# Where the sums for a Winograd aggregate are made: on GpSimd while the rows are at hand, or on VectorE from rows read back

## The chip, the cores and the metric

The kernel runs on one core of a Trainium2 chip. The metric is the device time of one execution in microseconds (us). The kernel before takes 3149.56 us, the median of three runs from 3143.49 to 3149.83 us; one further execution, taken with the hardware profiler, has a span of 3144.7 us, and its trace is what is read below.

## The reference, cut to what matters

Two graph layers on N = 2708 nodes with 1024 features. Only layer 0 is touched.

```python
h = jnp.maximum(_layernorm(x, axis=-1), 0.0)          # 2708 x 1024
f = h @ Wf + bf
g = h @ Wg + bg
e = relu(f @ g.T)
scores = where(adj > 0, e, NEG)                         # adj: 2708 x 2708 int32
attention = softmax(scores, axis=1)
x = x + (attention @ h) @ W + bW                        # the kernel's order of the two products
# layer 1: the same shape, with leaky_relu(f1 + f2.T) for e
```

So `h` is wanted twice: transposed, for the scores, and by rows, as one side of `attention @ h` ("the aggregate").

## The kernel before

Every large product is made by a Winograd form of Strassen's scheme: seven products of half-size blocks instead of eight. Each side of each product is a block or a sum of blocks. For the aggregate the row side is made of pairs of row tiles (a, b), each cut into two halves of 512 columns: `ha[0], ha[1], hb[0], hb[1]`. Seven operands come of it, stored in HBM as `hg_d[layer][group][:, m, j]`, with `m` in the order M1, M5, M6, M7, M3, M2, M4:

- M1, M2, M4 are plain halves: `ha[0]`, `hb[0]`, `hb[1]`;
- M5 = ha[1] + hb[1], M6 = M5 - ha[0], M7 = ha[0] - ha[1], M3 = hb[0] - M6 are sums.

Ten such pairs cover 20 of the 22 tiles. In the setup, while the products of the weights occupy TensorE, each pair is loaded, normalized, transposed, and:

```python
def stream(name, shape=(P, D), dt=FP):           # 12 buffers of 512 KB, for everything that streams
    return strm.tile(list(shape), dt, tag="strm", name=name)

def load(o, i):                                   # all loads: one queue (SyncE), kept in program order
    for a, b in in_16(o, i):
        tc.keep_in_program_order(nc.sync.dma_start(a, b))

def store(o, i):                                  # all stores: GpSimd's queue
    for a, b in in_16(o, i):
        nc.gpsimd.dma_start(a, b)

def pair_h(l, q, ha, hb):
    n = P
    on = nc.vector if l else nc.gpsimd
    g1, g2 = stream("g1", (P, 2, W)), stream("g2", (P, 2, W))
    s1, s2, s3, s4 = g1[:n, 0], g1[:n, 1], g2[:n, 0], g2[:n, 1]
    on.tensor_tensor(s1, ha[1], hb[1], OP.add)
    on.tensor_tensor(s2, s1, ha[0], OP.subtract)
    on.tensor_tensor(s3, ha[0], ha[1], OP.subtract)
    on.tensor_tensor(s4, hb[0], s2, OP.subtract)
    i, j = group_of[q]
    for m, h in ((M1, ha[0]), (M2, hb[0]), (M4, hb[1])):
        store(hg_d[l][i][:n, m, j], h)
    store(hg_d[l][i][:n, M5:M6 + 1, j], g1[:n])
    store(hg_d[l][i][:n, M7:M3 + 1, j], g2[:n])
```

Pieces of work that lie beside others are put on a list and taken from it a few at a time, `rate` us of estimated work after each product; what the next pieces load is fetched when they are among the first five of the list:

```python
later, credit = [], [0.0]
ahead = [5]
def put(us, go, fetch=None, takes_psum=False, ready=None): ...
def one():
    for it in later[:ahead[0]]:
        if it[1]:
            it[1]()                                # the fetch
            it[1] = None
    us, _, go = later.pop(0)[:3]
    go()
    return us
def behind(us, psum_free=False): ...               # one() until the credit is used up
```

After the weights' product M and the projection "q" of panel 0 come the first scores. For each pair q of ten, seven products of four matmuls each; the transposed operands are read from HBM, two products' worth per load, and the int32 adjacency for the pair after the next is fetched in eight small DMAs and made into a mask by VectorE:

```python
def product(q, m, ps, start):
    n, i = P, BY_SCORES.index(m)
    if i % 2 == 0:
        t = stream("As", (P, 2, NH, P))
        lefts[q] = t
        k = min(2, 7 - i)
        load(t[:, :k]..., hs_d[q][:, i:i + k]...)
    for c in range(NH):
        nc.tensor.matmul(ps[:n, :h], lefts[q][:, i % 2, c, :n], B[m][c // 2][:, c % 2, :h], ...)

nc.hold = ("vector",)                              # VectorE in program order during the scores
for q in range(NQ):
    make_until(q + 2)
    rate = 1.3 if NQ - 1 not in made else rates[p]      # rates[0] = 0.6
    if q + 2 <= LEFT:
        fetch(q + 2)                               # adj_i: stream("adj_i"), four DMAs; adj_t: four more
    ...
    product(q, M1, X, True)
    for s in (lo, hi):
        add(m1[:n, s], X[:n, :h], rb[:n, s])       # VectorE empties PSUM
    if left_over:
        left_over()                                # product M4 of the pair before
    product(q, M6, Z, True)
    add(t[:n, lo], Z[:n, :h], m1[:n, hi])
    behind(rate, True)
    ...                                            # M5, M2, M7, M3 alike; convert and turn the mask
```

The last pairs' normalization, transposes and sums for the scores run on into these first scores. The aggregate of panel 0 comes after the softmax and reads `hg_d`, 512 KB per load, into the same stream buffers.

Of the kernel before, what the change touches and what calls it, by code (L numbers as in the profile page):

```python
# [18 lines left out]
P = 128  # L19
W = 512  # L20
# [5 lines left out]
M1, M5, M6, M7, M3, M2, M4 = range(7)  # L26
# [31 lines left out]
def kernel(  # L58
# [19 lines left out]
    nc = InOrder(tc)  # L78
# [31 lines left out]
    NQ = len(pairs)  # L110
    pair_of = {t: (t // 2, t % 2) for t in range(MONO)}
    LEFT = NQ
# [15 lines left out]
    def stream(name, shape=(P, D), dt=FP):  # L128
        return strm.tile(list(shape), dt, tag="strm", name=name)

    def in_16(o, i):

        n = o.shape[0]
        k = n // 16 * 16
        return [(o, i)] if n in (k, 1) or not k or i.shape[0] != n else [(o[:k], i[:k]), (o[k:], i[k:])]

    def load(o, i):
        for a, b in in_16(o, i):
            tc.keep_in_program_order(nc.sync.dma_start(a, b))  # L139

    def store(o, i):
        for a, b in in_16(o, i):
            nc.gpsimd.dma_start(a, b)  # L143
# [11 lines left out]
    group_of = {q: (i, j) for i, g in enumerate(groups) for j, q in enumerate(g)}  # L155
    assert sorted(group_of) == list(range(NQ))
    hg_d = [[dram.tile([P, 7, len(g), W], FP, name=f"hg{l}_d{i}") for i, g in enumerate(groups)] for l in range(2)]
# [27 lines left out]
    def put(us, go, fetch=None, takes_psum=False, ready=None):  # L185
        later.append([us, fetch, go, takes_psum, ready])
# [4 lines that stand above are left out]
                it[1]()  # L191
# [4 lines that stand above are left out]
# [46 lines left out]
    def add(o, a, b):  # L242
        nc.vector.tensor_tensor(o, a, b, OP.add)

    def sub(o, a, b):
        nc.vector.tensor_tensor(o, a, b, OP.subtract)
# [42 lines left out]
    def left_h(l, hm, ht):  # L289

        for e in range(2):
            store(hgl_d[l][:, e, :W], hm[e])
            for d in range(NH):
                g = slice(B32 * d, B32 * (d + 1))
                store(hgl_d[l][g, e, W:], ht[e][g, d * P:(d + 1) * P])

    def pair_h(l, q, ha, hb):

        n = P
        on = nc.vector if l else nc.gpsimd  # L300
        g1, g2 = stream("g1", (P, 2, W)), stream("g2", (P, 2, W))
        s1, s2, s3, s4 = g1[:n, 0], g1[:n, 1], g2[:n, 0], g2[:n, 1]
        on.tensor_tensor(s1, ha[1], hb[1], OP.add)
# [5 lines that stand above are left out]
            store(hg_d[l][i][:n, m, j], h)  # L309
        store(hg_d[l][i][:n, M5:M6 + 1, j], g1[:n])  # L310
        store(hg_d[l][i][:n, M7:M3 + 1, j], g2[:n])

    u = consts.tile([P, NC], FP, name="u")
    v = consts.tile([P, NC], FP, name="v")
# [5 lines left out]
    def make_pairs():  # L320
        xs, hT = {}, {}

        def fetch(q):
            xs[q] = []
            for t in units[q]:
                xs[q].append(row_halves("x"))
                load_rows_of(t, xs[q][-1], x)

        def rows(q):
            left_h(0, *xs[q]) if q == LEFT else pair_h(0, q, *xs[q])  # L330

        def turned(q, k, e):
            t = units[q][k]
            ps = bank("h_ps", (P, NH, P))
            for c in range(NH):
                nc.tensor.transpose(ps[:, c, :], xs[q][k][e][:, c * P:(c + 1) * P], ident)
            for i, (s, n) in enumerate(pieces[0]):
                if s == t:
                    o = first_h[e].rearrange("p (c i) -> p c i", c=NH)[:, :, i * P:i * P + n]
                    nc.vector.tensor_copy(o, ps[:, :, :n])  # L340
            return ps

        def transposes(q):
            if q == LEFT:
                two = stream("hsl", (P, 2, NH, P))
                for e in range(2):
                    nc.scalar.copy(two[:, e], turned(q, 0, e))
                    nc.scalar.copy(tinyT[:, e], turned(q, 1, e)[:, :, :B32])
                store(hsl_d.rearrange("p e c j -> p (e c j)"), two.rearrange("p e c j -> p (e c j)"))
            else:  # L350
                ts = [stream("hsT", (P, 2, NH, P)) for _ in range(4)]
                hT[q] = ts, lambda i: ts[i // 2][:, i % 2]
                for k, e, i in ((0, 0, 0), (0, 1, 3), (1, 0, 7), (1, 1, 6)):
                    nc.scalar.copy(hT[q][1](i), turned(q, k, e))
            turned_tiles.update(units[q])

        def sums(q):
            if q == LEFT:
                return
            ts, i = hT.pop(q)  # L360
            at = {m: i(k) for k, m in enumerate(BY_SCORES)}
            add(at[M5], i(7), at[M4])
            sub(at[M6], at[M5], at[M1])
            sub(at[M7], at[M1], i(7))
            sub(at[M3], at[M2], at[M6])
            for g, t in enumerate(ts):
                store(hs_d[q][:, 2 * g:2 * g + 2].rearrange("p m c j -> p (m c j)"), t.rearrange("p m c j -> p (m c j)"))

        def dots(q, k):
            t = units[q][k]  # L370
            c = col_of[t]
            dot(r_[:, c:c + 1], xs[q][k], [vb[e][:, :W] for e in range(2)], c0)
            if t == MONO:
                nc.gpsimd.dma_start(r_[:NM, HALF:HALF + 1], r_[NM:, c:c + 1])

        def drop(q, what):
            seen.setdefault(q, set()).add(what)
            if len(seen[q]) == 3:
                xs.pop(q)

        def last(q):
            sums(q)
            drop(q, "sums")
            made.add(q)

        def bias(q, k):
            dots(q, k)
            drop(q, f"dots{k}")

        seen = {}  # L390
        def put_norms(q):
            put(2.1, lambda: normalize(xs[q][0]), lambda: fetch(q))
            put(2.1, lambda: normalize(xs[q][1]))

        put_rows = lambda q: put(0.5, lambda: rows(q))
        def put_dots(q):
            for k in range(2):
                put(1.6, lambda k=k: bias(q, k), ready=lambda: vb[0] is not None)

        todo = [0, 1, LEFT] + list(range(2, NQ))  # L400
        put_norms(todo[0])
        for i, q in enumerate(todo):
            if i + 1 < len(todo):
                put_norms(todo[i + 1])
            put_rows(q)
            put(0.5, lambda q=q: transposes(q), takes_psum=True)
            if i > 1:
                put_dots(q)
            put(2.7 if q != LEFT else 0.0, lambda q=q: last(q))
            if i == 1:  # L410
                put_dots(todo[0])
                put_dots(todo[1])

    def make_until(q):
        while min(q, NQ - 1) not in made:
            one()
# [110 lines left out]
    for name, gs in (("pick_lo", (0, 1)), ("pick_hi", (0, 2, 3))):  # L527
        t = consts.tile([P, P], FP, name=name)
# [228 lines left out]
        return r  # L757

    exps, LAG = [0], 2

    def exps_until(n):
        while exps[0] < n:
# [572 lines left out]
    for p in range(NP):  # L1335
        got["S"], got["acc"] = scores(p, B)
        generated[p] = NQ + 1
        ahead[0] = 2
        S = got["S"]
        hooks = {M1: lambda p=p: take_max(p), M2: lambda p=p: take_softmax(p)}  # L1340
        if p + 1 < NP:
            B = project_q(p + 1, hooks)
        else:
            nc.hold = ("vector",)
            project(0, p - 1, G.pop(p - 1), finish0(p - 1), hooks)
            nc.hold = ()
            scores_before()
        then = {M5: prepare_W} if p == 0 else {}
        if p == NP - 2:
            then[M2] = lambda: first_masks(NP - 1, 0)  # L1350
            then[M6] = lambda: first_masks(NP - 1, 1)
            then[M7] = lambda: first_masks(NP - 1, 2)
        G[p] = aggregate(0, p, S, got["sm"], then)
        if p == 0:
            flush()
            spread_wa()
        if p < NP - 2:
            project(0, p, G.pop(p), finish0(p), {M1: lambda p=p: first_masks(p + 1, 0),
                                                 M5: lambda p=p: first_masks(p + 1, 1),
                                                 M7: lambda p=p: first_masks(p + 1, 2)})  # L1360
# [88 lines left out]
    for p in range(NP):  # L1449
        S, sm = got["P"]  # L1450
        then = {}
        if p + 1 < NP:
            then = {M3: lambda p=p: take_shifts(p + 1), M7: lambda p=p: take_weights(p + 1)}
# [31 lines left out]
```

## Time and profile before

| what | figure |
|---|---|
| time, median of three runs | 3149.56 us |
| span of the profiled execution | 3144.7 us |
| TensorE busy | 3053.0 us (97% of the span) |
| VectorE busy | 1827.6 us (58%) |
| GpSimd busy | 462.8 us (15%) |
| ScalarE busy | 447.0 us (14%) |
| moved by DMA | 651.82 MB, 207 GB/s on average |
| granted TensorE clock | 0.990 |
| q of panel 0, start to end | 151.6 to 230.5 us |
| first scores | 231.2 to 399.7 us |

How to read it: TensorE works in nearly every slice of the span, so time can be won or lost mainly where it stands still. The shares are averages over stages with different limits, so the stages that the change touches, the setup (0 to 231 us) and the first scores, have to be looked at by themselves. One product of the scores is eight matmul records in the trace and takes 1.94 us; seven make one pair, 13.6 us.

### The profile page before, as it was taken

To read this page: it belongs to the slowest core of one execution; us is meant where nothing else is said; L and a number is where in the kernel's file an instruction comes from. 1 tells how busy PE (TensorE), PEld (TensorE's weight loads), DVE (VectorE), ACT (ScalarE), POOL (GpSimd) and SP (SyncE) were. 2 spreads that over 40 slices of the span, in tenths; PEclk is the share of its full clock that TensorE was granted. 3 is DMA by queue.
4 is the path that set the end of the run, shared out by engine and by line. 5 is a ranking of instruction groups with operands and counts; after the bars stand their busy time and mean duration, and the time that the engine had idled before them with its cause. 6 is when DMAs were issued, how large, how long until landed. Compare 5 with 4: busy or idle time off the path is not lost.

```text
span 3144.7 us, 36222 instructions
## 1 busy us (share of the span) xinstructions
PE 3053.0 (97%) x12712; PEld 2263.8 (72%) x12712; DVE 1827.6 (58%) x3730; ACT 447.0 (14%) x788; POOL 462.8 (15%) x664
## 2 busy tenths in 40 slices
PE   8988999999999999999999999997999999999998
PEld 4566777667877588876888885865757758678684
DVE  5867686286732687327881478658573471745612
ACT  3321020000200102001020002103031130211200
POOL 2643002210002100023000101020010020120102
PEclk9989999999999999999999999998999999999999
DMA  6888938878446796478945677686655565565655
GB/s 215 308 285 270 263 124 310 231 228 252 148 129 168 217 263 200 143 177 245 294 157 153 174 214 235 215 285 209 205 178 174 156 203 156 170 195 172 214 161 192
DMA packets 379045, 651.82 MB, mean 207 GB/s; under 512 B 170784, under 2 KB 211264, under 8 KB 378864
## 3 DMA queue, kind: packets, MB, share of 16 engines
q1 hardware_dynamic: 335920, 525.38, 55.7%
q0 software_dynamic: 42944, 124.13, 11.8%
q8 instruction: 101, 1.65, 0.2%
q14 instruction: 80, 0.66, 0.1%
HBM read 536.68 MB, written 112.67 MB: 206 GB/s over the span
## 4 chain that ended last, share of the span: by engine, by line
PE 83%; DMA 5%; issue 4%; DVE 4%; POOL 2%; SPq 1%; ACT 0%; POOLq 0%; DVEq 0%; ACTq 0%
PE gz L551 12%; PE gy L551 12%; PE gx L551 11%; PE sz L1061 7%; PE gv L551 5%; PE pz L953 5%; PE sy L1061 4%; PE sx L1061 4%; PE px L953 4%; PE py L953 4%; PE qz L551 3%; PE qy L551 2%; PE qx L551 2%; PE M_ps L467 2%; SPq L139 1%
## 5 line engine op out<-in xcount | busy, mean ns | idle before, releaser
L1061 PE MATMUL sz<-B,As 128*128 128x288 f32 (+2 forms) x1200 | 292.7, 393 | 8.2 <-DVE st L45 7.5
L1061 PEld LDWEIGHTS sz<-B,As 128*128 128x128 f32 x1200 | 227.7, 190 | 58.2 <-DVE st L45 11.9
L857 POOL TENSOR_TENSOR gT<-gT,rr 128x2304 f32<-128x2304 f32 (+5 forms) x20 | 72.7, 3635 | 1102.0 <-DVE rr L45 999.3
L1061 PE MATMUL sx<-B,As 128*128 128x288 f32 (+2 forms) x800 | 201.6, 395 | 13.2 <-DMA As<-hs_d 12.2
L1061 PE MATMUL sy<-B,As 128*128 128x288 f32 (+2 forms) x800 | 199.0, 392 | 0.0
L551 PE MATMUL gz<-P,hc 128*128 128x288 f32 (+2 forms) x800 | 186.0, 393 | 2.3 <-ACT gT L45 2.3
L551 PE MATMUL gz<-Sa,hc 128*128 128x288 f32 (+2 forms) x800 | 186.0, 393 | 2.3 <-ACT gT L45 2.3
L551 PE MATMUL gx<-P,hc 128*128 128x288 f32 (+2 forms) x800 | 186.1, 394 | 0.0
L1061 PEld LDWEIGHTS sx<-B,As 128*128 128x128 f32 x800 | 152.3, 191 | 45.4 <-DMA As<-hs_d 13.1
L551 PE MATMUL gy<-T,hc 128*128 128x288 f32 (+2 forms) x800 | 184.2, 391 | 0.0
L551 PEld LDWEIGHTS gz<-Sa,hc 128*128 128x128 f32 x800 | 151.2, 190 | 36.0 <-ACT gT L45 4.4
L551 PEld LDWEIGHTS gx<-P,hc 128*128 128x128 f32 x800 | 153.1, 192 | 32.8 <-issue 1.9
L551 PEld LDWEIGHTS gz<-P,hc 128*128 128x128 f32 x800 | 150.9, 190 | 35.6 <-ACT gT L45 4.4
L551 PEld LDWEIGHTS gy<-T,hc 128*128 128x128 f32 x800 | 152.0, 190 | 30.5
L1061 PEld LDWEIGHTS sy<-B,As 128*128 128x128 f32 x800 | 151.7, 190 | 30.6 <-DVE st L45 0.3
L953 PE MATMUL py<-w,ps 128*128 128x512 f32 x320 | 143.1, 597 | 4.7 <-DMA w<-in_L_gnn_W_dram 4.7
L953 PE MATMUL pz<-w,ps 128*128 128x512 f32 x320 | 142.8, 597 | 0.8 <-DVE pt L45 0.8
L953 PE MATMUL px<-w,gT 128*128 128x512 f32 x320 | 141.9, 596 | 0.7 <-issue 0.7
L143 POOL DMA_DIRECT2D out_dram<-x_res x180 | 88.9, 501 | 265.3 <-DVE x_res L45 259.0
L45 DVE TENSOR_TENSOR gT<-gy,u 128x288 f32<-128x288 f32 (+2 forms) x40 | 14.8, 431 | 183.5 <-PE gy L816 183.5
L953 PEld LDWEIGHTS py<-w,ps 128*128 128x128 f32 x320 | 60.5, 191 | 81.1 <-issue 77.5
L45 DVE TENSOR_TENSOR u<-gz,m 128x288 f32<-128x288 f32 (+2 forms) x40 | 17.6, 439 | 171.1 <-PE gz L551 170.7
(318 smaller groups left out, 5063.6 us busy)
## 6 DMA issues: line engine op xcount, KB each, us to landing
hc<-hg_d SPq DMA_DIRECT2D x350, 512.0 KB, 3.9
As<-hs_d SPq DMA_DIRECT2D x150, 512.0 KB, 5.8
w<-wt_d SPq DMA_DIRECT2D x96, 512.0 KB, 5.1
w<-in_L_gnn_W_dram SPq DMA_DIRECT2D x72, 512.0 KB, 4.3
md<-md_d SPq DMA_DIRECT2D x56, 512.0 KB, 4.6
adj_i<-in_adj_dram SPq DMA_DIRECT2D x200, 128.0 KB, 5.0
hg_d<-g POOLq DMA_DIRECT2D x40, 512.0 KB, 4.9
hs_d<-hsT POOLq DMA_DIRECT2D x40, 512.0 KB, 5.3
```

Of the source, the lines that this page charges most:

```text
L45: i = f(*a, **k)
L139: tc.keep_in_program_order(nc.sync.dma_start(a, b))
L143: nc.gpsimd.dma_start(a, b)
L467: nc.tensor.matmul(ps, wfT[a][c // NH][:, c % NH, :], wgT[b][c], start=(c == 0), stop=(c == NC - 1))
L551: nc.tensor.matmul(ps[d], left(m, k, d), right(m, k), start=(start and k == 0), stop=(k == K - 1 and m not in more), skip_group_check=True)
L857: nc.gpsimd.tensor_tensor(of(e, s), of(e, s), by(s, k), OP.mult)
L953: nc.tensor.matmul(ps, left[i][m][:, k, :], w_[k], start=(start and k == 0), stop=(k == NH - 1), skip_group_check=True)
L1061: nc.tensor.matmul(ps[:n, :h], lefts[q][:, i % 2, c, :n], B[m][c // 2][:, c % 2, :h], start=(start and c == 0), stop=(c == NH - 1), skip_g ...
```

## The change

The sums are no longer made when the rows are at hand. The setup only stores the four plain halves. Later, as the last entries of the list of pieces, each pair is read back from HBM (two loads of 512 KB into two stream buffers `hr`), VectorE makes the four sums in place, and three stores put them in `hg_d`. GpSimd is left with issuing stores. Before M5 of the first aggregate a call makes sure that no sum is outstanding.

```diff
     def pair_h(l, q, ha, hb):
         n = P
-        on = nc.vector if l else nc.gpsimd
+        on = nc.vector
@@
+    def rows_h(q, ha, hb):
+        i, j = group_of[q]
+        for m, h in ((M1, ha[0]), (M5, ha[1]), (M2, hb[0]), (M4, hb[1])):
+            store(hg_d[0][i][:, m, j], h)
+
+    summed = [0]
+
+    def sums_h():
+        def fetch(q, two):
+            i, j = group_of[q]
+            for m in (M1, M2):
+                two.append(stream("hr", (P, 2, W)))
+                load(two[-1], hg_d[0][i][:, m:m + 2, j])
+
+        def first(q, two):
+            (a0, a1), (b0, b1) = ((t[:, 0], t[:, 1]) for t in two)
+            add(b1, a1, b1)
+            sub(a1, a0, a1)
+
+        def second(q, two):
+            (a0, a1), (b0, b1) = ((t[:, 0], t[:, 1]) for t in two)
+            sub(a0, b1, a0)
+            sub(b0, b0, a0)
+            i, j = group_of[q]
+            store(hg_d[0][i][:, M6:M7 + 1, j], two[0])
+            store(hg_d[0][i][:, M3, j], b0)
+            store(hg_d[0][i][:, M5, j], b1)
+            summed[0] += 1
+        for q in range(NQ):
+            two = []
+            put(1.4, lambda q=q, two=two: first(q, two), lambda q=q, two=two: fetch(q, two))
+            put(1.4, lambda q=q, two=two: second(q, two))
@@ make_pairs
-            left_h(0, *xs[q]) if q == LEFT else pair_h(0, q, *xs[q])
+            left_h(0, *xs[q]) if q == LEFT else rows_h(q, *xs[q])
@@ make_pairs, after the loop over the pairs
+        sums_h()
@@
+    def sums_until_all():
+        while summed[0] < NQ:
+            one()
@@ before the aggregate of each panel
         then = {M5: prepare_W} if p == 0 else {}
+        if p == 0:
+            then[M1] = sums_until_all
```

It is for taking forty slow additions from GpSimd, which also issues every store of the setup in order, and for no longer making them beside VectorE's own work there.

## The prediction, made before the changed kernel ran

> **What bounds the kernel now.** First the shares by engine: TensorE is busy for 97% of the span and the chain that ended last is 83% TensorE, so I look for the places where TensorE stands still in the stages that the change touches, and for places where it might begin to. The busy time of each engine by stretches of 50 us finds them (columns: stretch, length, then busy us and count for TensorE's matmuls and weight loads, VectorE, ScalarE and GpSimd, the granted clock, the share of the DMA engines, GB/s):
>
> ```profile
> core 0: us, PE busy (x) PEld busy (x) DVE busy (x) ACT busy (x) POOL busy (x), PEclk, DMA share, GB/s
> 150.00:200.00 50.00, 34.29 (x127) 25.60 (x126) 39.06 (x73) 16.63 (x34) 30.91 (x43) 0.83 0.94 320
> 250.00:300.00 50.00, 37.19 (x158) 28.57 (x158) 34.93 (x79) 7.49 (x14) 20.42 (x25) 0.86 0.89 277
> 300.00:350.00 50.00, 50.00 (x207) 39.16 (x207) 31.90 (x69) 0.00 (x0) 2.17 (x4) 1.00 0.88 221
> 350.00:400.00 50.00, 50.00 (x230) 38.26 (x229) 29.14 (x59) 0.40 (x1) 1.62 (x3) 1.00 0.84 270
> ```
>
> TensorE stands still for 15.7 us and 12.8 us in two stretches; in the first scores after 300 us it never does. So all that the setup can give back is some 28 us. TensorE's timeline names the three large gaps (start, length, instruction, and in brackets the idle time before it and what ended it):
>
> ```profile
> 159.30 1.12 PE L336 MATMUL h_ps<-ident,x 128*128 128x128 f32 x4 [5.13 <-ACT M L45]
> 185.38 6.20 PE L551 MATMUL qx<-hT,M 128*128 128x288 f32 x16 [9.71 <-ACT m L45]
> 273.06 4.21 PE L1061 MATMUL sx<-B,As 128*128 128x288 f32 x8 [11.96 <-DMA As<-hs_d]
> ```
>
> What stands behind the first two is in the timelines of VectorE and GpSimd at that time:
>
> ```profile
> 152.59 4.41 DVE L45 SCALAR_TENSOR_TENSOR junk<-x,vb 128x512 bf16<-128x512 f32 x1
> 172.33 4.47 DVE L45 TENSOR_TENSOR hT<-hT,hT 128x1152 f32<-128x1152 f32 x1
> 191.62 1.36 DVE L45 TENSOR_TENSOR hT<-hT,hT 128x1152 f32<-128x1152 f32 x1 [4.76 <-PE qx L551]
> ...
> 152.73 1.28 POOL L303 TENSOR_TENSOR g<-x 128x512 f32<-128x512 f32 x1
> 171.86 1.28 POOL L303 TENSOR_TENSOR g<-x 128x512 f32<-128x512 f32 x1
> ```
>
> The same addition into hT takes 1.36 us alone and 4.47 us when GpSimd begins a group of sums at that moment; the dot with vb, 0.69 us elsewhere in this timeline, takes 4.41. ScalarE's next square root waits for VectorE's statistics, and the copies that TensorE waits for stand behind that square root.
>
> The third gap is in SyncE's queue of loads, which stands in program order (start, time in the queue, load, how many), read beside GpSimd's stores (first line):
>
> ```profile
> 257.90 1.48 POOL L143 DMA_DIRECT2D hg_d<-g  x2
> ...
> 261.19 3.83 SPq L139 DMA_DIRECT2D adj_i<-in_adj_dram  x4
> 265.07 2.39 SPq L139 DMA_DIRECT2D adj_t<-in_adj_dram  x4
> 267.56 9.86 SPq L139 DMA_DIRECT2D As<-hs_d  x4
> 302.46 3.08 SPq L139 DMA_DIRECT2D adj_i<-in_adj_dram  x4
> 305.59 4.21 SPq L139 DMA_DIRECT2D adj_t<-in_adj_dram  x4
> ```
>
> The adjacency load at 261.19 needs the stream buffer of a g tile, whose sums GpSimd finished just before its store at 257.90. Everything behind it in the queue waited, and the operands As came 12 us late.
>
> Last, how much room the first scores have. By pairs of tiles (same columns as above), and the landing time of the As loads from 220 to 400 us:
>
> ```profile
> 305.60:319.00 13.40, 13.40 (x57) 10.46 (x56) 8.52 (x19) 0.00 (x0) 0.50 (x1) 1.00 1.03 271
> 319.00:333.00 14.00, 14.00 (x59) 11.01 (x58) 9.10 (x19) 0.00 (x0) 0.58 (x2) 1.00 0.93 218
> 500.00:550.00 50.00, 46.04 (x187) 34.66 (x186) 42.27 (x118) 1.31 (x4) 13.51 (x25) 0.97 0.99 386
> DMA to landing us min/median/max: 3.8/6.2/9.1
> ```
>
> VectorE is two thirds busy, but the DMA engines are at 0.93 to 1.03 although they move only 218 to 271 GB/s; at 500 us, with long rows alone, the same share carries 386 GB/s. The rows of the adjacency, 256 bytes each, make the difference.
>
> **What the Trainium skill says.** "SBUF — State Buffer", section "Who interferes with whom": a VectorE instruction with two SBUF inputs and a GpSimd instruction that reads SBUF exclude each other, and the later one waits. The 4.47 us against 1.36 agree. "DMA: Bandwidth & Descriptors", "Why small descriptors are slow (HBM only)": a fixed cost for each descriptor weighs on short ones; the trace agrees (218 GB/s at a share of 0.93). The same page, "Issuing engines are not separate DMA queues": what GpSimd and SyncE issue runs on the same 16 engines. So moved stores and added loads compete with As; before shows the share, but not yet the competition. "Perfetto Trace Analysis", "Optimization Strategy": the same gap again and again on the engine that should be full can mean too few buffers. The scores before show no such gap; I expect it after.
>
> **Part by part: what is removed.** (a) Forty GpSimd sums of about 1.3 us, 52 us of GpSimd. Its time as such costs nothing; the exclusion does. The dot loses 4.41 - 0.69 = 3.7 us, the addition 4.47 - 1.36 = 3.1, and the dot after that (1.63 us in the timeline) 0.9. The 5.13 us gap should shrink by 3.7, the 9.71 us gap by 3.1 + 0.9 = 4.0: about 8 us. (b) The g tiles in the setup. In the changed program as built, the adjacency load of the third gap takes a buffer of transposed rows hsT instead. VectorE had finished those sums at 246.7 in the trace of before; the store was issued by 247.5, and hs_d stores land in 6.7 us (240 to 300 us), so the load may go at about 254 instead of 261: 7 us off the third gap. Together 15 us, with 28 as the ceiling.
>
> **What is added.** TensorE's order of instructions is the same. VectorE gets forty additions, 40 x 0.69 = 27.5 us, all placed in the first scores from the third pair to the tenth, 2.75 us a pair of sums, about 1.6 such pairs for each 13.6 us of TensorE: 9 + 4.5 = 13.5 us. That is the whole room, so VectorE alone is nearly the bound, but anything that slows TensorE there gives it room. I charge nothing extra for it.
>
> DMA: each pair is 1.05 MB read back and 1.05 MB stored, ten pairs 21 MB. At 386 GB/s that is 54 us of all engines. They fall on about six and a half pairs of the scores, 88 us of TensorE, in which the DMA engines are free for some 8%: 7 us. By this count the scores become 54 - 7 = 47 us longer. The stores taken from the setup (20 of 512 KB) don't help here: they are taken from a time when TensorE is limited by other things.
>
> Buffers: this is a second way to the same delay, so the two aren't added. The hr tiles take two of the twelve stream buffers per pair of sums and hold them through load, wait, two rounds of additions and store. In the program before, an As load becomes free to issue about twelve products ahead of its use (23 us); in the changed one, from the fourth pair to the ninth, most become free two or three products ahead (3.9 or 5.8 us). The queue in front of them has the eight adjacency loads, 3.1 + 4.2 = 7.3 us above, and As lands in 6.2 us or more. Walk through one pair: adjacency may issue at 0, is through at 7.3, As is issued and lands at about 14; TensorE wanted it at 5.9. That is 8 us. Another As of the same pair, two products ahead (3.9 us against 0.5 + 6.2), adds 1 to 3 us. Some 9 us a pair, six pairs: 54 us. Both ways give about 50; I take 48.
>
> Sum: 3149.6 - 15 + 48 = 3182.6; since adjacency may be quicker to issue once TensorE waits, and other small blocked VectorE instructions in the setup may give a little more, I say 3180.
>
> **The rivals.** (1) The gain as intended: sums are hidden, setup gives 15 to 25 us, time 3125 to 3135. For it: VectorE is only two thirds busy in the scores, and the middle of the scores has no gap at all, so there is a reserve of prefetch of 23 us to be eaten before TensorE feels anything. Against it: DMA at 0.93 to 1.03, and that the reserve is a matter of the buffers which hr takes. (2) Gain and loss about cancel, 3145 to 3160: the share of the DMA engines overstates how full they are (short rows keep an engine occupied without using its bandwidth), so that long rows slip in beside them. Then the loss is only the buffers' part, perhaps 20 us. (3) Worse: VectorE becomes the bound. It runs in program order in the scores; an addition that waits for a late hr load holds up the emptying of PSUM behind it, and DMA, VectorE and TensorE wait for each other in turn. Then 70 us or more are lost, 3205 to 3230.
>
> **Range and chances.** The loss, 48, may be from 20 to 75; the gain, 15, from 8 to 25. The outer combinations are 3145 and 3217; eight times in ten I expect 3150 to 3212. Two per cent are 63 us, so faster than 3086.6 has almost no chance (the ceiling of the gain is 28 us), and slower than 3212.5 needs rival 3: 0.12.
>
> **What would show it.** In the changed kernel's profile: VectorE's addition into hT in the setup near 1.4 us, and the gaps of 5.1 and 9.7 us shorter by about 4 each; the gap of 12 us about half; the first scores begin some 10 us sooner. In the scores: repeated gaps of TensorE before sx or sz, ended by the DMA As, of 3 to 10 us, from the fourth pair to the ninth, about 48 us in all; DMA share near 1 with over 300 GB/s; As landing at over 7 us in the median. If TensorE stays full in the scores, I am wrong on DMA and buffers; if its gaps are ended by VectorE, rival 3 holds; if the setup isn't shorter, the exclusion was not what held it up.

## The result and the profile after

| | before | changed |
|---|---|---|
| time, median of four runs (range) in us | 3148.61 (3143.49 to 3149.83) | 3184.28 (3180.71 to 3186.4) |
| ratio to before, 95% interval | | 1.0115 [1.0098, 1.0133] |
| profiled span | 3144.7 | 3180.5 |
| first product of the scores begins at | 231.24 | 211.49 |
| first scores, until q of the next panel begins | 168.35 | 221.66 |
| from there to the end | 2745.1 | 2747.35 |

The last three rows add up to the span and say where the time went: 19.75 us came out of the setup, 53.3 were lost in the first scores, 2.3 after them: +35.8.

In the setup, VectorE's timeline of the changed kernel has the two additions into hT (start, length, operation; idle before in brackets):

```profile
158.83 1.34 DVE L45 TENSOR_TENSOR hT<-hT,hT 128x1152 f32<-128x1152 f32 x1
171.87 1.36 DVE L45 TENSOR_TENSOR hT<-hT,hT 128x1152 f32<-128x1152 f32 x1 [2.71 <-PE qx L587]
```

Neither is blocked, where one took 4.47 us before. The busy time by stretches (columns as in the prediction) shows what TensorE makes of it, and what follows:

```profile
core 0: us, PE busy (x) PEld busy (x) DVE busy (x) ACT busy (x) POOL busy (x), PEclk, DMA share, GB/s
150.00:200.00 50.00, 50.00 (x220) 38.74 (x219) 30.81 (x66) 14.69 (x29) 11.31 (x22) 1.00 0.79 252
250.00:300.00 50.00, 28.28 (x95) 20.80 (x96) 24.71 (x53) 0.00 (x0) 6.88 (x12) 0.80 0.85 272
300.00:350.00 50.00, 36.47 (x129) 26.84 (x128) 26.70 (x52) 0.00 (x0) 6.55 (x11) 0.86 0.83 262
350.00:400.00 50.00, 33.97 (x121) 25.16 (x120) 26.52 (x52) 0.00 (x0) 6.55 (x11) 0.83 0.78 247
```

From 150 to 200 us TensorE is full, 50.0 against 34.3 us. From 250 on it stands still for a third of the time, its clock drops to 0.80 to 0.86, and the DMA engines are no busier than in the kernel before (0.89 and 0.88 from 250 to 350 us there). TensorE's timeline has twelve gaps in the scores, 53.0 us in all, of 0.8 to 10.6 us; some of them:

```profile
255.86 3.68 PE L1101 MATMUL sy<-B,As 128*128 128x288 f32 x8 [6.70 <-DMA As<-hs_d]
275.96 3.88 PE L1101 MATMUL sx<-B,As 128*128 128x288 f32 x8 [10.60 <-DMA As<-hs_d]
305.28 2.21 PE L1101 MATMUL sy<-B,As 128*128 128x288 f32 x8 [0.83 <-DMA As<-hs_d]
320.10 3.99 PE L1101 MATMUL sx<-B,As 128*128 128x288 f32 x8 [6.79 <-DMA As<-hs_d]
341.88 4.21 PE L1101 MATMUL sx<-B,As 128*128 128x288 f32 x8 [4.24 <-DMA As<-hs_d]
...
390.54 4.21 PE L1101 MATMUL sx<-B,As 128*128 128x288 f32 x8 [8.50 <-DMA As<-hs_d]
```

Eleven of the twelve are ended by the DMA As, one by VectorE's mask. After each of the seven gaps of 4.05 us and more the next eight matmuls take 3.6 to 4.2 us instead of 2.2: such a gap costs its length and then 1.4 to 2.0 us more. The chain of waits shows how one gap comes about (start, length, what):

```profile
292.52 0.54 POOL mk_d L143
293.09 6.86 DMA hg_d<-hr
300.00 5.23 DMA As<-hs_d
305.28 2.22 PE sy L1101 x8
...
307.90 0.83 DVE nm L45 x2
...
309.00 0.48 SPq L139
309.53 1.00 SPq L139
...
313.90 6.16 DMA As<-hs_d
...
320.10 3.99 PE sx L1101 x8
```

And SyncE's queue in the same stretch (start, time in the queue, load):

```profile
300.00 1.36 SPq L139 DMA_DIRECT2D As<-hs_d  x2
302.54 2.31 SPq L139 DMA_DIRECT2D hr<-hg_d  x2
308.61 2.45 SPq L139 DMA_DIRECT2D adj_i<-in_adj_dram  x4
311.11 2.69 SPq L139 DMA_DIRECT2D adj_t<-in_adj_dram  x4
313.90 1.39 SPq L139 DMA_DIRECT2D As<-hs_d  x3
315.39 11.04 SPq L139 DMA_DIRECT2D hr<-hg_d  x2
```

Read from below: TensorE wanted As for its product sx at about 313; it was only issued at 313.90, behind eight adjacency loads that took 5.1 us to issue. Those could not start before 308.6, when VectorE's `nm` had finished with the adjacency before it and freed its buffer, and that waited for the product sy, which waited for an As at 300.00, which waited for the store of an `hr` tile to give back a buffer. The store itself stood in GpSimd's queue behind the store of a mask. Each late As delays what frees the buffer for the next one. Last, the landing times from 240 to 400 us (bytes of one load, median us to landing):

```profile
As<-hs_d SPq DMA_DIRECT2D x23, 512.0 KB, 5.5
hr<-hg_d SPq DMA_DIRECT2D x18, 512.0 KB, 6.4
```

As lands faster than in the kernel before (7.0 us in the same stretch). It isn't slow on the way; it is sent late.

### The profile page after: what moved, and what is told of

Same layout as the page of the kernel before. It is cut to its first block, busy times and chain, and to the rows that moved or that the text cites. A ratio compares the mean times of both kernels' runs of the same rounds, so it can differ in the third digit from the quotient of the medians.

```text
span 3180.5 us, 36350 instructions
## 1 busy us (share of the span) xinstructions
PE 3060.7 (96%) x12712; PEld 2272.7 (71%) x12712; DVE 1827.1 (57%) x3770; ACT 447.6 (14%) x788; POOL 420.4 (13%) x644
## 4 chain that ended last, share of the span: by engine, by line
PE 85%; DMA 5%; DVE 4%; issue 3%; SPq 2%; POOL 1%; ACT 0%; DVEq 0%; POOLq 0%; ACTq 0%
PE gz L587 12%; PE gy L587 11%; PE gx L587 11%; PE sz L1101 6%; PE pz L993 5%; PE gv L587 5%; PE sy L1101 4%; PE sx L1101 4%; PE px L993 4%; PE py L993 4%; PE qz L587 3%; PE M_ps L503 3%; PE qy L587 2%; PE qx L587 2%; SPq L139 2%
## 5 line engine op out<-in xcount | busy, mean ns | idle before, releaser
L1101 PE MATMUL sx<-B,As 128*128 128x288 f32 (+2 forms) x800 | 210.9, 409 | 42.4 <-DMA As<-hs_d 40.8
L587 PEld LDWEIGHTS gz<-P,hc 128*128 128x128 f32 x800 | 151.2, 190 | 35.3 <-ACT gT L45 4.4
L993 PEld LDWEIGHTS pz<-w,ps 128*128 128x128 f32 x320 | 60.9, 192 | 78.1 <-issue 72.6
```

Source lines behind the costliest of these rows:

```text
L587: nc.tensor.matmul(ps[d], left(m, k, d), right(m, k), start=(start and k == 0), stop=(k == K - 1 and m not in more), skip_group_check=True)
L993: nc.tensor.matmul(ps, left[i][m][:, k, :], w_[k], start=(start and k == 0), stop=(k == NH - 1), skip_group_check=True)
```

## The experiments

The theories: **buffers** (the hr tiles hold stream buffers, so As is issued late), **bytes** (21 MB more fill the DMA engines), **VectorE** (its 27 us more, or its waits for hr, hold up the emptying of PSUM), and for the setup **exclusion** (GpSimd's sums hold up VectorE) or something else. All ratios are to the kernel before, run on the same chip; three lengths of each profiled run follow in a table at the end of this section.

**No sums.** The call of the sums is left out; the setup stores plain rows in the places of M6, M7 and M3, so that as many planes are written. Its output lacks the sums.

```diff
-        for m, h in ((M1, ha[0]), (M5, ha[1]), (M2, hb[0]), (M4, hb[1])):
+        for m, h in ((M1, ha[0]), (M5, ha[1]), (M2, hb[0]), (M4, hb[1]), (M6, ha[0]), (M7, ha[1]), (M3, hb[0])):
@@
-        sums_h()
```

> No sums at all in layer 0: the setup stores plain rows in all seven planes (the same bytes as the kernel before), no g tiles, nothing is read back. It shows the gain alone. If the exclusion of VectorE by GpSimd and the g buffers were all of it: scores start some 20 us sooner and the gap of 12 us in the scores goes, 3113 to 3122 us. If the setup was shortened by fewer stores (a megabyte a pair moved out of it): 3135 to 3149, as the stores are back.

Measured: 3121.02 us (3117.38 to 3125.16), ratio 0.9916 [0.9902, 0.9931]. So the gain by itself is 27 us and the sums with all they bring cost 63 (3184.28 - 3121.02). By the profiled lengths the first scores are 62.4 us shorter (221.66 - 159.28) and the rest 1.1, but the scores begin 4.8 us later, at 216.3. That is a cost of this kernel itself: all seven planes of a pair can be stored as soon as its rows are at hand, fourteen stores of 256 KB from 15 to 60 us where the changed kernel has eight; in that time TensorE waits 2.47 us for a load of Wf, and q begins at 157.67 instead of 152.87 us. The three kernels here that store seven planes of plain rows begin q at 155.2 to 157.7 us, all others at 151.2 to 154.1. From q to the scores this kernel and the changed one both take 58.6 us. So the gain of 27 us is, if anything, some 5 too small, and the loss is best read as 62.4 us in the scores. From 240 to 400 us TensorE is all but full:

```profile
240.00:400.00 160.00, 155.34 (x668) 119.92 (x667) 105.71 (x222) 14.13 (x27) 10.75 (x20) 0.99 0.82 241
```

**Short additions.** The four additions work on 8 of the 512 columns; reads, stores, buffers and order stay.

```diff
-            add(b1, a1, b1)
-            sub(a1, a0, a1)
+            add(b1[:, :8], a1[:, :8], b1[:, :8])
+            sub(a1[:, :8], a0[:, :8], a1[:, :8])
@@ the other two alike
```

> The changed kernel with the forty additions on 8 of 512 columns (the other sums are left out): loads, stores and buffers as they are, 27 us less of VectorE in the scores. VectorE theory: the loss goes, 3120 to 3135 us. Buffers and DMA theories: nearly as the changed kernel, 3170 to 3186.

Measured: 3185.91 us (3181.81 to 3186.33), ratio 1.0119 [1.0104, 1.0134]: as the changed kernel. The costliest groups in the scores (count, then busy us and mean ns) of the changed kernel and of this one:

```profile
L45 DVE TENSOR_TENSOR hr<-hr 128x512 f32<-128x512 f32 x40 | 27.3, 683 | 0.7
```

```profile
L45 DVE TENSOR_TENSOR hr<-hr 128x8 f32<-128x8 f32 x40 | 6.3, 158 | 0.7
```

Twenty-one us less of VectorE shorten the scores by 0.8 us. So VectorE's work is not what makes the loss of the changed kernel; whether it would cost something once As came in time, this run doesn't show. In the changed kernel it is VectorE that waits for TensorE (46.4 us for sx alone from 220 to 450 us).

**Buffers and bytes, two by two.** One kernel keeps the bytes and puts the rows into buffers of another pool (54 slots of 256 KB), so that no stream buffer is taken:

```diff
-            for m in (M1, M2):
-                two.append(stream("hr", (P, 2, W)))
-                load(two[-1], hg_d[0][i][:, m:m + 2, j])
+            for m in (M1, M5, M2, M4):
+                two.append(slot("hr")[:, :W])
+                load(two[-1], hg_d[0][i][:, m, j])
@@ four stores of 256 KB instead of one of 512 and two of 256
```

> The rows are read back into buffers of the other pool (four of 576 columns for a pair) instead of two stream buffers; bytes, additions and their place are the same. Buffers theory (As loads come late because hr tiles hold stream buffers): most As loads are again eight to ten products ahead of their use, the gaps before sx go, 3120 to 3135 us. DMA theory (21 MB more than the engines can carry in the scores): no change, 3175 to 3190. VectorE theory: no change either, 3175 to 3190.

Another keeps the stream buffers and reads, adds and stores only 16 of the 128 partitions, an eighth of the bytes; the rest of M6, M7 and M3 are plain rows stored in the setup:

```diff
+        R = 16
@@
-                load(two[-1], hg_d[0][i][:, m:m + 2, j])
+                load(two[-1][:R], hg_d[0][i][:R, m:m + 2, j])
@@ additions and stores on [:R] alike
```

> The changed kernel, but read back, summed and stored on 16 of the 128 partitions only (the sums of the others are left out, and the setup stores plain rows in the three planes that would have no data): an eighth of the bytes, the same additions in length, the same stream buffers, two or three products from a free buffer to the use of As. DMA theory: the loss goes, 3115 to 3130 us. Buffers theory: most of the loss stays, since the distance is the same and only the store of hr lands sooner: 3155 to 3180. VectorE theory: 3175 to 3190.

The third does both:

> Both suspected costs taken away together: rows read back into the other pool's buffers, on 16 of 128 partitions (the other sums left out, plain rows stored in the setup in the planes without data); the additions keep their length on VectorE. If buffers and bytes are the whole loss, the scores go back to the 159 us that they take without any sums, and the time is that of the kernel without sums: 3118 to 3127 us. If VectorE's additions or the longer queues cost something of their own, 3130 to 3145.

Measured: slots 3157.67 us (3152.52 to 3161.97), ratio 1.0031 [1.0019, 1.0043]; 16 rows 3173.35 (3172.95 to 3174.08), 1.0083 [1.0066, 1.01]; both 3140.29 (3135.82 to 3143.9), 0.9973 [0.9962, 0.9985]. The lengths of the first scores:

| first scores, us | all rows | 16 of 128 rows | bytes cost |
|---|---|---|---|
| in stream buffers | 221.7 | 204.1 | 17.6 |
| in slots | 193.8 | 175.9 | 17.9 |
| stream buffers cost | 27.9 | 28.2 | |

Against 159.3 without sums, the 62.4 us fall into 28 for the buffers, 18 for the bytes, and 17 that are left with both away. So buffers and bytes add up, and no theory alone fits: for slots the buffers' theory expected at most 3135 us, the others at least 3175. The two rows agree more closely than the measurement allows, though. Each length is that of one profiled execution, and that of slots was the fastest of its six (3152.52 us, median 3157.67). By the medians of the whole time the buffers cost 26.6 and 33.1 us, the bytes 10.9 and 17.4; the kernels with 16 rows lose part of their gain elsewhere, as the table at the end shows (scores begin some 2 and 6 us later, the rest is 6 and 1.5 us longer). From 240 to 400 us, slots and 16 rows:

```profile
240.00:400.00 160.00, 130.12 (x526) 97.60 (x525) 107.57 (x213) 2.45 (x5) 29.87 (x56) 0.94 1.03 339
```

```profile
240.00:400.00 160.00, 119.99 (x456) 89.91 (x455) 103.35 (x210) 3.70 (x8) 24.92 (x48) 0.90 0.67 196
```

With the buffers freed the DMA engines are busy all the time, share 1.03 at 339 GB/s, and As lands in 9.3 us; this is the picture that the prediction had drawn of the changed kernel. With few bytes they are at 0.67 and As lands in 4.5 us, and TensorE still stands for 40 us, always for As. The remaining 17 us are not separated: with both, SyncE still issues forty more loads in the scores at about 0.44 us each (four in 1.76 us, 17.6 in all; in stream buffers it is twenty, of twice the size) and waits 16.4 us for stores of hr, and VectorE still makes its additions (26.8 us, 16 partitions take as long as 128). Each of these, and the eighth of the bytes that is left, may have a part in it.

**Two milder ways to free buffers.** The rows are fetched when their sums are among the first three of the list instead of five, so that they hold their buffers for a shorter time; or there are fourteen stream buffers and 50 slots:

```diff
+            ahead[0] = 3                           # in the first kernel, in the fetch of the sums
@@
-    slots = ctx.enter_context(tc.tile_pool(name="slots", bufs=54))
-    strm = ctx.enter_context(tc.tile_pool(name="strm", bufs=12))
+    slots = ctx.enter_context(tc.tile_pool(name="slots", bufs=50))   # in the second
+    strm = ctx.enter_context(tc.tile_pool(name="strm", bufs=14))
```

> The changed kernel with the same bytes, the same sums and the same twelve stream buffers; only the rows are read back when their sums are among the first three entries of the list instead of the first five, so an hr tile holds its buffer for a shorter time. In the program as built the As loads then become free to issue four or five products ahead of their use instead of two or three. If buffers make most of the loss: the scores shrink from 221.7 us to some 195 to 205, the time to 3155 to 3168 us. If bytes make it: nothing changes, 3180 us or more. If it is the wait for the rows themselves (VectorE now reads them sooner after their load): gaps ended by VectorE, and 3185 us or more.

> The changed kernel with fourteen stream buffers instead of twelve, paid for with four of the 54 slots of 256 KB; bytes, sums and the order of the loads stay. As loads become free four or five products ahead. If buffers make most of the loss: 3155 to 3170 us, with DMA above 285 GB/s in the scores where the changed kernel shows 247 to 272. If bytes make it: 3180 us. The fewer slots could cost something elsewhere; then the scores are shorter and the rest of the kernel longer.

Measured: fetched at three 3160.21 us (3157.25 to 3161.44), ratio 1.0038 [1.0023, 1.0053]; fourteen buffers 3149.74 (3146.48 to 3153.12), 1.0007 [0.9998, 1.0016]. With all bytes and all sums the scores shrink to 199.4 and 202.0 us, as buffers say. The 3149.74 are not the scores alone: the rest of that kernel is 11 us shorter too (2736.3 against 2747.35), and 9 of these are gaps of 3.1, 1.1 and 4.8 us before later operands from HBM, which the changed kernel has and which are all but gone. The kernel before was not run with fourteen buffers, so its 3147 us is no fair base for this one. The stretch from 240 to 400 us with fourteen buffers:

```profile
240.00:400.00 160.00, 125.12 (x465) 93.91 (x464) 103.86 (x209) 2.05 (x4) 27.19 (x46) 0.88 0.95 309
```

Again the transfers move up, from 269 to 309 GB/s, as soon as buffers are to be had.

**Adjacency out of the queue.** The adjacency loads of panel 0 are issued by ScalarE, so that As doesn't stand behind them:

```diff
-                load(t[B32 * g:B32 * (g + 1), :, k] ...
+                (load if p else lambda o, i: tc.keep_in_program_order(nc.nc.scalar.dma_start(o, i)))(t[B32 * g:B32 * (g + 1), :, k] ...
```

> The changed kernel with the adjacency loads of panel 0 issued by ScalarE instead of SyncE; As no longer stands behind eight small DMAs in one queue. This tests one term of the prediction: adjacency through the queue at 7.3 us, then As. If that term carries the gaps of about 10 us (issue 5.1 us in the changed kernel's trace, seven pairs): up to 35 us of the loss goes, 3150 to 3165 us. If As is late because its own buffer comes free late, the queue in front matters little: 3172 to 3186 us. ScalarE has little to do in the scores, so that its own queue should hold nothing up.

Measured: 3180.74 us (3176.89 to 3181.59), ratio 1.0102 [1.0087, 1.0117], scores 221.0 us. The sum is unchanged, but not the places: from 300 to 400 us TensorE is busy for 81.7 us (changed kernel: 70.4), from 200 to 300 for 68.7 (76.6). ScalarE's timeline shows what was lost early (ACTq is its queue of DMA issues):

```profile
254.79 7.25 ACTq L713 DMA_DIRECT2D adj_i<-in_adj_dram  x2
265.91 2.64 ACTq L713 DMA_DIRECT2D adj_t<-in_adj_dram  x4
268.65 2.05 ACT L45 COPY hsT<-h_ps 128x512 f32<-128x512 f32 x4 [13.46 <-DMA adj_t<-in_adj_dram]
```

ScalarE's copies of the last transposed pairs now stand behind adjacency loads that wait for a buffer, and As needs what those copies make. Here the expectation was wrong that ScalarE's queue holds nothing up. So the wait was moved, not removed, and how much of the loss is owed to the adjacency's place in the queue stays open: the eleven us between 300 and 400 speak for a part, the total for none.

**The gain alone: VectorE in the setup.** The kernel before with one word changed; the sums stay where they were.

```diff
-        on = nc.vector if l else nc.gpsimd
+        on = nc.vector
```

> The kernel before with one word changed: the sums are made at the same place, into the same g tiles, by VectorE instead of GpSimd. If it was the exclusion between the two engines that held up the setup, VectorE gets faster by more than its 27 us more work over 180 us cost: the scores begin 12 to 20 us sooner, and the gap of 12 us in the scores is smaller too, since VectorE has its sums sooner; 3120 to 3135 us. If the engine didn't matter, but the g tiles did, 3145 to 3155, or more, as VectorE gets fuller.

Measured: 3131.58 us (3128.6 to 3133.83), ratio 0.9946 [0.9931, 0.996]: 17 us faster than before and 53 faster than the change. TensorE's gaps from 120 us to the end of the scores:

```profile
171.74 5.73 PE L551 MATMUL qx<-hT,M 128*128 128x288 f32 x16 [3.16 <-ACT m L45]
248.09 4.15 PE L1061 MATMUL sz<-B,As 128*128 128x288 f32 x16 [0.52 <-DVE Sb L45]
261.61 4.18 PE L1061 MATMUL sy<-B,As 128*128 128x288 f32 x8 [7.62 <-DMA As<-hs_d]
274.01 2.21 PE L1061 MATMUL sx<-B,As 128*128 128x288 f32 x8 [1.67 <-DMA As<-hs_d]
```

The gap of 5.13 us is gone and that of 9.71 is 3.16, with VectorE doing all forty sums there (0.68 us each in the timeline). VectorE had the room for the sums in the setup itself. That the two engines held each other up fits: the additions into hT take 1.34 and 1.36 us here. But the sums also no longer stand in front of the stores in GpSimd's queue, and this run doesn't tell the two apart.

**The g tiles in slots**, with VectorE and with GpSimd making the sums in the setup (four `slot("g")` and four stores of 256 KB in layer 0 instead of g1 and g2):

> As the run before, and the sums go into buffers of the other pool (four of 576 columns) instead of two stream buffers. Exclusion and g buffers both gone: 3118 to 3130 us; about 8 us under the run before if the g buffers had their own part, the same if not.

> The kernel before with its sums on GpSimd as they were, into buffers of the other pool instead of stream buffers. Only the g buffers' part of the gain: the gap of 12 us in the scores goes, the setup's gaps stay: 3132 to 3142 us. If the g tiles weren't the cause of that gap: 3145 to 3150.

Measured: VectorE 3131.6 us (3130.41 to 3131.92), ratio 0.9946 [0.9931, 0.996]; GpSimd 3136.41 (3135.57 to 3137.0), 0.9962 [0.9948, 0.9976]. The stream buffers of the g tiles alone are worth some 12 us, the engine alone 17, and both together no more than 17: once the g tiles are in slots, the engine adds only 5. The expectation that the setup's gaps stay with GpSimd was wrong in part. The scores begin 7.1 us sooner; the gap of 5.13 us is gone, that of 9.71 is 4.14, and one of 5.07 us before qz, ended by ScalarE, is new. GpSimd's sums fall at other times there, and the addition into hT takes 1.87 us, not 4.47.

**The best with the adjacency elsewhere.** VectorE in the setup, and the adjacency issued by ScalarE:

> The kernel before with VectorE making the sums in the setup (3131.6 us) and the adjacency loads of panel 0 issued by ScalarE. The remaining gap of 7.6 us before sy, ended by As, stands behind adjacency in the queue. If the queue is the cause: 3122 to 3127 us. If not, or if ScalarE's copies in the setup's tail stand behind an adjacency load that waits for its buffer: 3131 to 3140 us.

Measured: 3148.12 us (3142.74 to 3155.47), ratio 1.0001 [0.9992, 1.0009], 16.5 us slower than without it. The gaps become 12.49 and 8.27 us; ScalarE's copies stand behind adjacency again (8.24 us before two of them). A miss, and the same lesson as above.

| profiled run | scores begin | first scores | rest |
|---|---|---|---|
| before | 231.2 | 168.4 | 2745.1 |
| changed | 211.5 | 221.7 | 2747.4 |
| no sums | 216.3 | 159.3 | 2746.2 |
| short additions | 211.7 | 220.9 | 2747.4 |
| slots | 209.8 | 193.8 | 2747.1 |
| 16 rows | 213.8 | 204.1 | 2753.3 |
| slots, 16 rows | 216.1 | 175.9 | 2748.6 |
| fetched at three | 212.7 | 199.4 | 2747.6 |
| fourteen buffers | 210.0 | 202.0 | 2736.3 |
| adjacency by ScalarE | 211.0 | 221.0 | 2747.6 |
| VectorE in the setup | 216.6 | 165.5 | 2744.7 |
| the same, g in slots | 220.0 | 161.8 | 2748.3 |
| GpSimd, g in slots | 224.2 | 163.4 | 2746.1 |
| VectorE in the setup, adjacency by ScalarE | 216.5 | 179.8 | 2744.7 |

## Why the prediction was right, point by point

**The time** was right, 3180 said and 3184.28 measured, inside the range and on the side named. The kind of gain and the kind of loss were right too: VectorE no longer held up in the setup, TensorE waiting for late As in the scores. The two terms of the sum, however, were both too small, by 12 and by 15 us; that these errors cancelled is luck.

**The gain, 15 said, 27 shown** (no sums). The exclusion shows in the instructions, the addition into hT went from 4.47 to 1.36 us, and moving the sums off GpSimd alone gave 17 us, of which its share isn't separated from that of GpSimd's queue of stores. The step that was mis-sized is "the gaps of 5.1 and 9.7 us shorter by about 4 each". I took only the blocked time of the instructions named, but both gaps closed entirely (15.7 us of TensorE standing from 150 to 200 us became none), and with them went some 5 us of slow matmuls behind the gaps (6.20 us for sixteen became 4.12, one of the groups). From q to the scores 79.6 us became 58.6; q itself began 1.2 us later, so the scores began 19.75 us sooner, not 10. The 7 us off the third gap were about right: without sums the scores are 9 us shorter than before. That the stores taken from the setup don't help was right from q on: 58.6 us to the scores with seven planes stored and with four.

**The loss, 48 said, 63 shown.** By the buffers' account, gaps of TensorE ended by As were to be 54 us; 51.2 were there (53.0 with the one ended by the mask), and the walk through one pair can be read in the chain: adjacency, then As, then TensorE, with 5.1 us for the adjacency instead of 7.3 and 6.16 for As. That the sizes meet is luck in part: 4.7 us of gaps are there without sums as well, and with the buffers given back the scores became only 28 us shorter, since TensorE still waited for As, which then landed in 9.3 us. What the account left out is the clock: seven gaps of 4.05 us and more were each followed by eight matmuls of 3.6 to 4.2 us, some 13 us together. The Trainium skill, "TensorE: Matmul & The Clock Gate", section "Part 1: The HAM clock gate", describes just this, a TensorE that runs at half speed for a while after standing still; the trace agrees (4.21 us against 2.10 for a product after a long gap), and the figure had been in the profile of before, in the line of the 12 us gap.

**"Two ways to the same delay, so the two aren't added"** was wrong. Measured two by two, buffers cost about 28 and bytes about 18 in the scores, and 17 more are left with both away. They do add up, and each alone had been put far too high, at 54 us the buffers and at 54 - 7 = 47 the bytes. The weak step of the bytes' account is the 8% of free DMA time. It was read from two pairs of tiles (1.03 and 0.93), while the lines for 300 to 400 us show 0.88 and 0.84; and the share overstates how full the engines are, as rival 2 had it: without sums a share of 0.82 carried 241 GB/s from 240 to 400 us, with slots 1.03 carried 339.

**DMA share near 1, over 300 GB/s, As landing at over 7 us** was wrong for the changed kernel: 0.78 to 0.85, 247 to 272 GB/s, 5.5 us. A queue that waits for buffers can't fill the engines. All three signs appeared when buffers were freed (slots: 1.03, 339 GB/s, 9.3 us).

**VectorE charged with nothing** was right for the changed kernel (short additions: no difference), and with it rival 3 falls. It had more room than I counted, because TensorE's standing still gives it time. **Rival 1** had the setup's gain right, 15 to 25 us, against my own 15, and the reserve of prefetch wrong: the buffers that make that reserve are the ones the rows take. **Rival 2**, 3145 to 3160, is where the kernels that free buffers end up (3149.7 to 3160.2).

**Where the gain of the intent lies**: 17 of the 27 us come from the engine alone and need no reading back. VectorE in the setup, at 3131.58 us, beats both kernels. Beside it, the change begins the scores 5 us sooner (211.5 against 216.6) and makes them 56 us longer (221.7 against 165.5).

## What to carry to other kernels

When a change moves work into a stage that looks roomy, count first which buffers it takes from the prefetch there and how long it holds them; an empty engine and a DMA share below 1 don't help a load that is issued late. Split a change into what frees (here another engine) and what pays (here the reading back), and run the free half by itself: one word was worth 17 us, and the rest of the change lost 53. Charge a gap of several us on TensorE with the slow matmuls behind it too; they were there after every gap of 4.05 us and more of the changed kernel, while with 16 rows in stream buffers two gaps of 3.71 and 3.79 us had none.

## What the hardware showed that I had not expected

- **Buffers and bytes cost separately**: in the scores of the profiled executions 27.9 and 28.2 us for the buffers, 17.6 and 17.9 for the bytes, whichever of the other held.
- **The landing time of As doesn't tell how long TensorE waits for it**: with 16 rows in stream buffers As landed in 4.5 us and TensorE's gaps in the scores were 39.9 us; with all rows in slots it landed in 9.3 us and the gaps were 30.8.
- **Moving eight small DMAs a pair to an idle engine's queue** made the best kernel 16.5 us slower: ScalarE's copies waited up to 13.46 us (in the changed kernel's variant) behind loads that waited for a buffer.
- **A blocked VectorE instruction can wait for a run of GpSimd's sums.** In the kernel before, the addition of 4.47 us ended at 176.80 us. GpSimd's timeline after the sum at 171.86:

```profile
173.10 1.26 POOL L305 TENSOR_TENSOR g<-x 128x512 f32<-128x512 f32 x1
174.32 1.26 POOL L304 TENSOR_TENSOR g<-g,x 128x512 f32<-128x512 f32 x1
176.11 1.82 POOL L306 TENSOR_TENSOR g<-x,g 128x512 f32<-128x512 f32 x1
```

Its own 1.36 us fit just behind the third sum, which ended at 175.58, and the fourth sum took 1.82 us instead of 1.27. The dot of 4.41 us, from 152.59 to 157.00, stood beside three sums from 152.73 to 156.44 in the same way. It isn't always so: a dot at 109.47 us took 1.85 us and waited for one sum only.
